# Gated cross-attention and mixture of experts: the query projection packed eight heads at a time, the second MLP layer in halves, and a new order of the side pieces

## The chip, the cores and the metric

The kernel runs on one core of one Trainium2 chip. The metric is the device time of one execution in microseconds (us), smaller is better. Each number below is from that core.

## The reference

Four batches of 512 tokens with 256 features attend to a context of 1601 rows with 192 features; 16 heads of 16 dimensions. Then a routed feed-forward layer follows. Cut to what matters:

```python
q = (layernorm(x) @ Wq + bq).reshape(B, N, 16, 16)
k = (y @ Wk + bk).reshape(B, M, 16, 16);  v = (y @ Wv + bv).reshape(B, M, 16, 16)
attn = softmax(einsum('bnhd,bmhd->bhnm', q, k) / 4)
out = einsum('bhnm,bmhd->bnhd', attn, v).reshape(B, N, 256)
x = x + tanh(g_xattn) * (relu(out @ W1 + b1) @ W2 + b2)      # W1 256x512, W2 512x256
x = x + tanh(g_ffn) * (shared expert + 2 of 8 routed experts)(layernorm(x))
```

All of it is float32.

## The kernel before

**Units and steps.** The attention works on 16 units: unit i = 4 * batch + group, where a group is four heads. A group's four heads lie on the 128 partitions in four slots of 32 partitions, 16 of them used (`HS` = 32, `HD` = 16). The keys come in 13 tiles of 128 rows (the last has 65), so there are 13 steps (i, kt) per unit, 208 steps in all, written out by hand in `step` (L622). A step holds:

- a first burst: two score matmuls of the tile after this one (`score`, L421) and two matmuls of the maxima of the unit after this one (`maximum`, L362). ScalarE takes the exponentials (`exponent`, L430), VectorE the row maxima (`reduce_max`, L373; L375 for the short last one, which falls into step kt = 10).
- the sum over values of this tile (`add_values`, L442), four heads.
- at kt = 11, where a new unit's maxima are complete, VectorE joins them (`negate`, L395), TensorE turns them (`turn_neg`, L408), and VectorE adds them to the queries (`qA_add`, L416).
- a second burst, for the other heads.
- the late work `late[s]`: side pieces that prepare the next batch or finish the last one.

The order on TensorE, ScalarE, VectorE and SyncE is the program's order (`manual_schedule`). Of PSUM's eight banks three serve the scores (`ps_sc`), three the maxima (`ps_mx`), one the sum over values, and one the side pieces (`ps_ms`, `side()`). A burst uses two of the three banks for maxima, so the second maximum of a burst needs the bank that the first reduction of the burst before it empties.

**Side pieces.** `make_q` (L289) projects the queries of one unit: the weights `wq_t` are laid out with gaps, 32 columns for a head's 16, so one unit fills 128 columns. It runs as two halves of 256 tokens, each two matmuls, and ScalarE adds the bias into `qT`. `make_k` (L306) projects keys for eight heads at once into `kd`, 16 partitions for a head, in four chunks, and `spread` (L322) brings four heads by four DMAs on SyncE's queue to their slots in one of three fixed tiles `ks`. `make_v` (L333) projects one tile of values. `normalize` (L453), `make_oT` (L475), `make_xnT` (L280) and `route` parts 0 and 1 (L518) are four transposes each; `route` part 2 is 16 small matmuls. `mlp_in` (L485) is the first layer in halves of 256 tokens, `mlp_out` (L500) the second, for 128 tokens at a time: eight matmul instructions on 256 output columns, then an addition on VectorE into `ys`. `residual` (L513) updates x and takes the statistics on VectorE. `rstd_of` (L236) starts with three small operations on VectorE and goes on on GpSimd, as `apply` (L259) does.

**The plan.** `put` (L551) assigns a piece to a step, by hand. A step that gets TensorE work is in `large`. A step with none (and not at kt = 0 or 11) has its sum over values cut into two halves (`halves`, L628), the second of them after the second burst. Last, the four warm-up pieces of values run in steps before the table, and 13 rounds of maxima of unit 0 run before the steps (L684), with the loads of `other_loads` (L197) issued in between.

After the steps the last batch is finished beside the shared expert, then the routed experts run in tiles of 128 pairs (L1040).

Of the kernel before, what the change touches and what calls it, by code (L numbers as in the profile page):

```python
# [9 lines left out]
FP = mybir.dt.float32  # L10
AF = mybir.ActivationFunctionType
# [15 lines left out]
def kernel(  # L27
# [117 lines left out]
    sp1 = xattn.enter_context(tc.tile_pool(name="sp1", bufs=1, side="right"))  # L145
    esp = xattn.enter_context(tc.tile_pool(name="esp", bufs=10, side="right"))
    wq_t = sp1.tile([P, 2, G * P], FP, name="wq_t")
    wk_t = sp1.tile([KC + 1, 2, NH * HD], FP, name="wk_t")
    wv_t = sp1.tile([KC + 1, 2, G * P], FP, name="wv_t")

# [6 lines left out]
    ctx_t = sp1.tile([KC + 1, 2, M], FP, name="ctx_t")  # L157
    nc.vector.memset(ctx_t[KC : KC + 1, 1, :], 1.0)
    ks = [sp1.tile([P, M], FP, name=f"ks_{n}") for n in range(3)]
    vs = [sp1.tile([P, NH, HS], FP, name=f"vs_{n}") for n in range(NKT + 2)]  # L160
    neg = sp1.tile([P, NTB, HPG, HS], FP, name="neg")
    for t in ks:
# [32 lines left out]
        nc.sync.dma_start(out=wv_t[:KC], in_=wv.rearrange("(c p) n -> p c n", p=KC))  # L195

    def other_loads():  # L197
        for b in range(1, B):
            load_x(b)
        for h in range(NH):  # L200
            nc.sync.dma_start(
                out=w1_t[h * HD % P : h * HD % P + HD, h * HD // P, :],
                in_=w1[h * HS : h * HS + HD, :],
            )
        nc.sync.dma_start(out=b1_t, in_=b1)
        nc.sync.dma_start(out=w2_t, in_=w2.rearrange("(c p) n -> p c n", p=P))
        nc.sync.dma_start(out=b2_t, in_=b2.partition_broadcast(P))
        nc.sync.dma_start(out=rb_t, in_=rb.partition_broadcast(P))
        nc.sync.dma_start(out=ord_t, in_=order.partition_broadcast(P))
        nc.sync.dma_start(out=wr_t, in_=wrT.rearrange("(c p) e -> p c e", p=P))  # L210
# [11 lines left out]
    mv2 = const.tile([P, NT // P, 2], FP, name="mv2")  # L222
    rstd2 = const.tile([P, NT // P], FP, name="rstd2")
    xnT, qT, qA, mxs = {}, {}, {}, {}
    kd, hid, oT, toks, ys = {}, {}, {}, {}, {}

    def side():
        return ps_ms.tile([P, S], FP, tag="ms", name="ms")
# [57 lines left out]

        return slice(0, S) if h is None else slice(h * S // 2, (h + 1) * S // 2)

    def make_q(i, h=None, ps=None):  # L289
        b, g = divmod(i, G)  # L290
        ps = side() if ps is None else ps
        n = half_of(h)
        for c in range(2):
            nc.tensor.matmul(  # L294
                ps[:, n],
                lhsT=wq_t[:, c, g * P : (g + 1) * P],
                rhs=xnT[b][:, c, n],
                start=(c == 0),
                stop=(c == 1),
            )  # L300
        if not h:
            qT[i] = sp2.tile([P, S], FP, tag="qT", name=f"qT_{i}")
            mxs[i] = sp2.tile([P, NTB, HPG, NCH], FP, tag="mxs", name=f"mxs_{i}")
        nc.scalar.activation(qT[i][:, n], ps[:, n], AF.Identity, bias=bq_t[:, g : g + 1])

    def make_k(b, h2, part, ps=None):  # L306
        if part == 0:
# [189 lines left out]
            )  # L497
        nc.scalar.activation(hid[b][:, f, n], ps[:, n], AF.Relu, bias=b1_t[:, f : f + 1])

    def mlp_out(b, t):  # L500
        ps = side()
        for f in range(NF):
            nc.tensor.matmul(  # L503
                ps[:, :H],
                lhsT=hid[b][:, f, t * P : (t + 1) * P],
                rhs=w2_t[:, f, :],
                start=(f == 0),
                stop=(f == NF - 1),
            )
        ys[b, t] = p2.tile([P, H], FP, tag="y", name=f"y_{b}_{t}")  # L510
        nc.vector.tensor_tensor(ys[b, t], ps[:, :H], b2_t, ALU.add)

    def residual(b, t):  # L513
        xt = xs[b][:, t, :]
# [34 lines left out]
    large = set()  # L549

    def put(where, i, kt, work, *args):  # L551
        if where is late and work not in (spread, load_ctx, load_expert, stats1, rstd_of, apply, residual):
            large.add(i * NKT + kt)
        where[i * NKT + kt].append(lambda: work(*args))


    for i in range(NG):
        b, g = divmod(i, G)
        nb = b + 1 if b + 1 < B else None
        if i:  # L560
            put(late, i, 1, normalize, i - 1)
        if g == 0:
            if b:
                for part, kt in enumerate((0, 2, 3, 4)):
                    put(late, i, kt, make_k, b, 1, part)
                put(late, i, 4, spread, i + 2)
                for h2 in range(2):
                    put(late, i, 5 + h2, make_oT, b - 1, h2)
            put(late, i, 7, make_q, i + 2, 0)
            put(late, i, 8, make_q, i + 2, 1)  # L570
            if b:
                for n in range(4):
                    put(late, i, 9 + n, mlp_in, b - 1, n // 2, n % 2)
            if nb:
                put(late, i, 5, load_ctx, nb)
                for t in range(NTB):
                    put(late, i, 6 + t, stats1, nb, t)
        if g == 1:
            put(late, i, 0, spread, i + 2)
            if b:  # L580
                for n, kt in enumerate((0, 2, 3, 4)):
                    put(late, i, kt, mlp_in, b - 1, 2 + n // 2, n % 2)
                for t in range(NTB):
                    put(late, i, 5 + t, mlp_out, b - 1, t)
                    put(late, i, 6 + t, residual, b - 1, t)
                put(late, i, 9, rstd_of, b - 1, mv2, rstd2, nc.gpsimd)
            put(late, i, 9, make_q, i + 2, 0)
            put(late, i, 10, make_q, i + 2, 1)
            if nb:
                put(late, i, 9, rstd_of, nb, mv1, rstd1, nc.gpsimd)  # L590
                put(late, i, 11, make_k, nb, 0, 0)
                put(late, i, 12, make_k, nb, 0, 1)
            if b:
                put(late, i, 9, apply, b - 1, mv2, rstd2, nc.gpsimd)
            if nb:
                put(late, i, 9, apply, nb, mv1, rstd1, nc.gpsimd)
                put(late, i, 8, load_expert, 0, w_sh) if b == 0 else None
        if g == 2:
            if nb:
                put(late, i, 0, make_k, nb, 0, 2)  # L600
                put(late, i, 2, make_k, nb, 0, 3)
                put(late, i, 2, spread, i + 2)
                for c in range(2):
                    put(late, i, 5 + c, make_xnT, nb, c)
                put(late, i, 8, make_q, i + 2, 0)
                put(late, i, 9, make_q, i + 2, 1)
                put(late, i, 10, make_v, nb, 0)
                put(late, i, 11, make_v, nb, 1)
                put(late, i, 12, make_q, i + 3, 0)
            if b:  # L610
                for part, kt in enumerate((3, 4, 7)):
                    put(late, i, kt, route, b - 1, part)
        if g == 3 and nb:
            put(late, i, 0, spread, i + 2)
            put(late, i, 0, make_q, i + 2, 1)
            for kt in range(2, NKT):
                put(late, i, kt, make_v, nb, kt)

    for kt in range(NKT - NCH, NKT):
        put(late, 0, kt - (NKT - NCH) - 2, make_v, 0, kt)  # L620
# [35 lines left out]
    with tc.manual_schedule(  # L656
        engines={
            mybir.EngineType.PE,
            mybir.EngineType.Activation,
            mybir.EngineType.DVE,  # L660
            mybir.EngineType.SP,
        }
    ):
        first_loads()
        for c in range(2):
            r = slice(0, KC + c)
            nc.scalar.copy(
                wk_t[r, c, :].rearrange("p (h d) -> p h d", d=HD),
                wk_slots[r, c, :].rearrange("p (h d) -> p h d", d=HS)[:, :, :HD],
            )  # L670
        for t in range(NTB):
            stats1(0, t)
        rstd_of(0, mv1, rstd1, nc.vector)
        apply(0, mv1, rstd1, nc.vector)
        for part in range(NCH):
            pool, tag = (ps_mx, "mx") if part == NCH - 1 else (ps_sc, "sc")
            make_k(0, 0, part, ps=pool.tile([P, S], FP, tag=tag, name="k0"))
        spread(0, (nc.sync, nc.scalar, nc.sync, nc.sync))
        make_k(0, 1, 0)
        for c in range(2):  # L680
            make_xnT(0, c, ps_mx.tile([P, S], FP, tag="mx", name="xnT0"))
        make_q(0, ps=ps_sc.tile([P, S], FP, tag="sc", name="q0"))
        spread(1)
        for u in range(NKT):  # L684
            banks = [(ps_mx, "mx") if j % 2 else (ps_sc, "sc") for j in range(HPG)]
            for bank in run([(maximum, reduce_max, (0, u), j, *banks[j]) for j in range(HPG)]):
                bank()
            if u == 0:
                make_q(1)
            elif u < NCH:  # L690
                make_k(0, 1, u)
            else:
                make_v(0, u - NCH)
            if u == NCH:
                spread(2)
                other_loads()
                nc.scalar.activation(tg, gt, AF.Tanh)
        for s in range(-2, LAST + 1):
            step(s)
    xattn.close()  # L700
# [515 lines left out]
```

## Time and profile before

| What | us |
|---|---|
| median of three runs | 1247.69 (1246.52 to 1248.03) |
| the profiled execution's own time | 1245.65 |
| its span, first to last instruction | 1243.9 |
| granted TensorE clock, mean | 0.999 |
| stretch of the steps | 54.2 to about 918 |
| TensorE busy in the span | 1222.9 |
| VectorE busy / ScalarE busy | 683.1 / 587.0 |

The span is 1.75 us shorter than the execution's own time, and that execution was 2.04 us faster than the median of the runs. Busy time of TensorE counts from an instruction's start to its modelled end, so matmuls that wait within a burst can still look busy; the starts of the next group tell how long a group really held the engine. In the timeline a row is: start in us, length in us, engine, line, operation, out<-in, form, count, and in brackets the idle time before it and what ended it. In the groups by line and shape a row ends with busy us, mean ns of one | idle us before.

### The profile page before, as it was taken

What the parts mean: (1) busy time and instruction counts of PE and PEld (TensorE: products, weight loads), DVE (VectorE), ACT (ScalarE), POOL (GpSimd) and SP (SyncE); (2) the same over time, 40 slices, a digit from 0 to 9 for tenths busy, and PEclk for the clock granted to TensorE, in tenths of its full rate; (3) what the DMA queues carried; (4) which work ended last, traced back from release to release, by engine and by line L of the source; (5) the groups of instructions that cost most, each with busy time, mean ns of one, the idle gap of its engine ahead of it and who ended that gap; (6) DMA issues with size and microseconds to landing.
All of it is one profiled execution on the core that took longest, in us unless ns stands there. A gap on an engine that the chain in (4) does not pass through costs nothing.

```text
span 1243.9 us, 19394 instructions
## 1 busy us (share of the span) xinstructions
PE 1222.9 (98%) x7654; PEld 544.1 (44%) x7654; DVE 683.1 (55%) x1287; ACT 587.0 (47%) x1127; POOL 129.0 (10%) x208
## 2 busy tenths in 40 slices
PE   7999999999999999999999999999999999999997
PEld 3533334333343433343434333343336656666664
DVE  5967666656666566666666665677304721121126
ACT  2265656556545555555565556545661122222220
POOL 2000110000004000000400000020000033333320
PEclk9999999999999999999999999999999999999999
DMA  5312000002000100120010001000047011111106
GB/s 125 103 41 65 1 15 15 1 1 54 14 2 4 29 14 1 27 41 1 1 31 15 1 1 17 11 1 18 1 152 271 1 35 39 46 46 40 44 23 207
DMA packets 30752, 48.29 MB, mean 39 GB/s; under 512 B 5247, under 2 KB 21505, under 8 KB 30662
## 3 DMA queue, kind: packets, MB, share of 16 engines
q1 hardware_dynamic: 26628, 38.14, 11.7%
q0 software_dynamic: 3504, 8.40, 2.1%
q8 instruction: 62, 1.02, 0.3%
q10 hardware_dynamic: 530, 0.50, 0.1%
q14 instruction: 28, 0.23, 0.1%
HBM read 32.86 MB, written 8.78 MB: 33 GB/s over the span
## 4 chain that ended last, share of the span: by engine, by line
PE 94%; DVE 2%; issue 1%; DMA 1%; ACT 0%; POOL 0%; SPq 0%; POOLq 0%; DVEq 0%; ACTq 0%
PE sc L421 32%; PE av L442 17%; PE gp L998 5%; PE up L998 5%; PE y_ps L1016 5%; PE mx L362 4%; PE ms L339 4%; PE ms L313 3%; PE ms L491 3%; PE ms L294 3%; PE ms L503 2%; PE up L721 1%; PE gp L721 1%; PE th L1009 1%; PE op L744 1%
## 5 line engine op out<-in xcount | busy, mean ns | idle before, releaser
L373 DVE TENSOR_REDUCE mxs<-mx 128x1 f32<-128x512 f32 x744 | 479.8, 685 | 251.1 <-PE mx L362 247.3
L430 ACT ACTIVATE es<-sc 128x512 f32<-128x512 f32 x804 | 437.7, 594 | 340.9 <-PE mx L362 291.3
L362 PE MATMUL mx<-ks,qT 32*128 32x512 f32 (+1 forms) x1984 | 480.6, 549 | 0.0
L421 PE MATMUL sc<-qA,ks 32*128 32x512 f32 x1608 | 467.6, 637 | 0.8 <-DVE qA L416 0.8
L421 PEld LDWEIGHTS sc<-qA,ks 32*128 32x128 f32 x1608 | 131.2, 179 | 221.8 <-issue 165.3
L442 PE MATMUL av<-es,vs 128*32 128x512 f32 (+2 forms) x1864 | 227.8, 559 | 0.1
L362 PEld LDWEIGHTS mx<-ks,qT 32*128 32x128 f32 x1984 | 164.7, 183 | 4.0 <-issue 1.9
L442 PEld LDWEIGHTS av<-es,vs 128*32 128x32 f32 (+1 forms) x1864 | 37.1, 108 | 166.2 <-issue 161.2
L1052 DVE TENSOR_TENSOR hid<-sg,up 128x512 f32<-128x512 f32 x35 | 24.1, 688 | 124.2 <-PE up L998 124.2
L244 POOL TENSOR_SCALAR var<-var 128x4 f32<-128x4 f32 x6 | 1.4, 238 | 782.8 <-DVE first L241 782.8
L1050 ACT ACTIVATE sg<-gp 128x512 f32<-128x512 f32 x35 | 20.9, 598 | 103.8 <-PE gp L998 103.8
L998 PE MATMUL gp<-w_all,xT 128*128 x140 | 66.0, 594 | 0.9 <-ACT xT L994 0.9
L1016 PE MATMUL y_ps<-w_all,hT 128*128 x280 | 66.2, 379 | 0.0
L998 PE MATMUL up<-w_all,xT 128*128 x140 | 65.9, 593 | 0.0
L339 PE MATMUL ms<-wv_t,ctx_t 96*128 96x256 f32 (+1 forms) x208 | 58.7, 404 | 0.1
L1016 PEld LDWEIGHTS y_ps<-w_all,hT 128*128 128x128 f32 x280 | 50.6, 190 | 5.9 <-issue 0.5
L339 PEld LDWEIGHTS ms<-wv_t,ctx_t 96*128 96x128 f32 (+1 forms) x208 | 34.5, 185 | 37.9 <-issue 27.3
L1025 POOL DMA_INDIRECT rows_y<-y,dest x35 | 35.6, 1017 | 131.0 <-DVE y L1024 131.0
L313 PE MATMUL ms<-ctx_t,wk_t 96*128 96x401 f32 (+3 forms) x112 | 45.1, 524 | 0.0
L978 POOL DMA_INDIRECT xg<-rows_x,token x38 | 39.2, 1031 | 48.1 <-DVE token L962 36.7
L737 ACT ACTIVATE sg<-gp 128x512 f32<-128x512 f32 x16 | 9.6, 597 | 62.7 <-PE gp L721 52.5
L375 DVE TENSOR_REDUCE mxs<-mx 128x4 f32<-128x260 f32 x62 | 23.8, 424 | 26.4 <-PE sc L421 22.6
(165 smaller groups left out, 943.9 us busy)
## 6 DMA issues: line engine op xcount, KB each, us to landing
ks<-kd SPq DMA_DIRECT2D x63, 100.1 KB, 3.2
w_all<-in_wgT SPq DMA_DIRECT2D x8, 512.0 KB, 11.1
w_all<-in_wuT SPq DMA_DIRECT2D x8, 512.0 KB, 10.0
w_all<-in_wdT SPq DMA_DIRECT2D x8, 512.0 KB, 11.2
w_all<-rows_y SPq DMA_DIRECT2D x8, 512.0 KB, 8.4
ctx_t<-in_ctxT SPq DMA_DIRECT2D x3, 1200.8 KB, 8.1
xb<-in_x SPq DMA_DIRECT2D x4, 512.0 KB, 6.2
rows_x<-xn SPq DMA_DIRECT2D x4, 512.0 KB, 3.4
```

Source lines behind the costliest of these rows:

```text
L294: nc.tensor.matmul(ps[:, n], lhsT=wq_t[:, c, g * P : (g + 1) * P], rhs=xnT[b][:, c, n], start=(c == 0), stop=(c == 1),)
L313: nc.tensor.matmul(ps[:, :n], lhsT=wk_t[r, c, h2 * P : (h2 + 1) * P], rhs=ctx_t[r, c, o : o + n], start=(c == 0), stop=(c == 1),)
L339: nc.tensor.matmul(ps[:n, : NH * HD], lhsT=ctx_t[r, c, o : o + n], rhs=heads[r, c, :, :HD], start=(c == 0), stop=(c == 1),)
L362: nc.tensor.matmul(ps[:, n * REST : (n + 1) * REST] if last else ps, lhsT=qT[i][slot_of(j), qb * P : (qb + 1) * P], rhs=ks[i % 3][slot_of( ...
L373: nc.vector.tensor_reduce(mxs[i][:, qb, j, c : c + 1], ps, AX.X, ALU.max)
L421: nc.tensor.matmul(ps[:n, :], lhsT=ks[i % 3][r, o : o + n], rhs=qA[i][r, :], start=True, stop=True)
L430: nc.scalar.activation(es[(i * NKT + kt) % 2, j][:n], ps[:n], AF.Exp, scale=SCALE)
L442: nc.tensor.matmul(av[i][j * HS : (j + 1) * HS, cols], lhsT=v_of(b, kt)[:n, g * HPG + j, :], rhs=es[(i * NKT + kt) % 2, j][:n, cols], star ...
L491: nc.tensor.matmul(ps[:, n], lhsT=w1_t[:, c, f * P : (f + 1) * P], rhs=oT[b][:, c, n], start=(c == 0), stop=(c == 1),)
L978: nc.gpsimd.indirect_dma_start(out=xg[i % 4], out_offset=None, in_=rows_x, in_offset=bass.IndirectOffsetOnAxis(ap=token[:, i : i + 1], axi ...
L998: nc.tensor.matmul(ps, lhsT=xT[i][:, c, :], rhs=w_flat[:, bass.ds(owners[i] + (off + c) * I, I)], start=(c == 0), stop=(c == 1),)
L1016: nc.tensor.matmul(ps, lhsT=hT2[i][:, f, :], rhs=w_flat[:, bass.ds(owners[i] + 4 * I + f * H, H)], start=(f == 0), stop=(f == NI - 1),)
```

## The change

The weights of the queries are also kept without gaps: `wq_d`, 256 columns for 16 heads, is made from `wq_t` by two ScalarE copies in the warm-up, and `bq_d`, its bias, is loaded by two more DMAs. Units 0 and 1 are still projected from `wq_t` (`first_q`). All others go through `make_q(b, h2, h)`, which projects eight heads at once into `qd`, and `spread_q`, which sends four heads by four DMAs on SyncE's queue to their slots in one of two fixed tiles `qs`. The gaps in `qs` keep the zeros that `first_q` wrote. `mlp_out` runs in two halves of 128 output columns where the plan calls it (the last batch, after the steps, keeps it whole). The plan of side pieces of a batch is written anew.

```diff
-    def make_q(i, h=None, ps=None):
-        b, g = divmod(i, G)
...
+    def make_q(b, h2, h):
+
+        ps = side()
         n = half_of(h)
         for c in range(2):
             nc.tensor.matmul(
                 ps[:, n],
-                lhsT=wq_t[:, c, g * P : (g + 1) * P],
+                lhsT=wq_d[:, c, h2 * P : (h2 + 1) * P],
                 rhs=xnT[b][:, c, n],
...
+    def spread_q(i):
+        b, g = divmod(i, G)
+        home_of(i)
+        for j in range(HPG):
+            r = (g % 2 * HPG + j) * HD
+            nc.sync.dma_start(
+                out=qT[i][j * HS : j * HS + HD, :], in_=qd[b, g // 2][r : r + HD, :]
+            )
...
-    def mlp_out(b, t):
+    def mlp_out(b, t, h=None):
         ps = side()
+        n = slice(0, H) if h is None else slice(h * H // 2, (h + 1) * H // 2)
         for f in range(NF):
             nc.tensor.matmul(
-                ps[:, :H],
+                ps[:, n],
                 lhsT=hid[b][:, f, t * P : (t + 1) * P],
-                rhs=w2_t[:, f, :],
+                rhs=w2_t[:, f, n],
...
-        nc.vector.tensor_tensor(ys[b, t], ps[:, :H], b2_t, ALU.add)
+        if not h:
+            ys[b, t] = p2.tile([P, H], FP, tag="y", name=f"y_{b}_{t}")
+        nc.vector.tensor_tensor(ys[b, t][:, n], ps[:, n], b2_t[:, n], ALU.add)
...
+    for b in range(B):
+        i = b * G
         nb = b + 1 if b + 1 < B else None
+        mlp = [(mlp_in, b - 1, n // 2, n % 2) for n in range(2 * NF)]
+        outs = [(mlp_out, b - 1, n // 2, n % 2) for n in range(2 * NTB)]
...
+        put_all(i, (7, 8), [(make_q, b, 1, h) for h in range(2)])
+        put(late, i, 8, spread_q, i + 2)
+        put(late, i + 1, 0, spread, i + 3)
+        put(late, i + 1, 2, spread_q, i + 3)
+        if b and nb:
+            put_all(i, (9, 10, 11, 12), mlp[:4])
+            put_all(i + 1, (0, 2, 3, 4), mlp[4:])
+            at = [(i + 1, 5 + n) for n in range(2 * NTB)]
+        elif b:
+            put_all(i, (9, 10, 12), mlp[:3])
+            put_all(i + 1, (0, 2, 3, 4, 5), mlp[3:])
+            at = [(i + 1, kt) for kt in (6, 7, 8, 9, 10, 12)] + [(i + 2, 0), (i + 2, 2)]
+        if b:
+            for n, (k, kt) in enumerate(at):
+                put(late, k, kt, *outs[n])
+                if n % 2:
+                    put(late, *divmod(k * NKT + kt + 1, NKT), residual, b - 1, n // 2)
+            k, kt = divmod(k * NKT + kt + 1, NKT)
+            put(late, k, kt, rstd_of, b - 1, mv2, rstd2, nc.gpsimd)
+            put(late, k, kt, apply, b - 1, mv2, rstd2, nc.gpsimd)
+            put_all(i + 2, (9, 10, 12) if nb else (8, 9, 10), [(route, b - 1, n) for n in range(3)])
...
+            put(late, i + 1, 3, rstd_of, nb, mv1, rstd1, nc.gpsimd)
+            put(late, i + 1, 3, apply, nb, mv1, rstd1, nc.gpsimd)
...
+            put_all(i + 2, (0, 2, 3, 4), [(make_k, nb, 0, part) for part in range(NCH)])
+            put(late, i + 2, 4, spread, i + 4)
+            put_all(i + 2, (5, 6), [(make_xnT, nb, c) for c in range(2)])
+            put_all(i + 2, (7, 8), [(make_q, nb, 0, h) for h in range(2)])
+            put(late, i + 2, 8, spread_q, i + 4)
+            put(late, i + 3, 0, spread, i + 5)
+            put(late, i + 3, 2, spread_q, i + 5)
...
+                for c in range(2):
+                    nc.scalar.copy(
+                        wq_d[:, c, :].rearrange("p (h d) -> p h d", d=HD),
+                        wq_t[:, c, :].rearrange("p (h d) -> p h d", d=HS)[:, :, :HD],
+                    )
```

Values keep their 13 pieces a batch: in batches 1 and 2 the first one moves from (i + 2, 10) to (i + 2, 11) and the second from there to (i + 3, 0); in batch 0 they fill (i + 2, 9), (i + 2, 10) and all of unit i + 3 but steps 1 and 11.

## The prediction

> **What bounds the kernel.** I read the page's busy table first, then the chain that ended last, then the groups by line and shape, then the timeline of TensorE in steps of each kind.
>
> ```profile
> PE 1222.9 (98%) x7654; PEld 544.1 (44%) x7654; DVE 683.1 (55%) x1287; ACT 587.0 (47%) x1127; POOL 129.0 (10%) x208
> ...
> PE 94%; DVE 2%; issue 1%; DMA 1%; ACT 0%; POOL 0%; SPq 0%; POOLq 0%; DVEq 0%; ACTq 0%
> ```
>
> TensorE (PE) is busy 98% and holds 94% of the chain: time goes where its instructions go, unless a wait hides inside a burst. So I price whole steps, by starts in its timeline. One step of unit 5 (rows of L362 left out):
>
> ```profile
> 354.46 0.69 PE L421 MATMUL sc<-qA,ks 32*128 32x512 f32 x1
> ...
> 355.53 1.06 PE L442 MATMUL av<-es,vs 128*32 128x512 f32 x8
> 356.52 0.69 PE L421 MATMUL sc<-qA,ks 32*128 32x512 f32 x1
> ...
> 357.60 1.99 PE L503 MATMUL ms<-w_t,hid 128*128 128x256 f32 x8
> 359.52 0.69 PE L421 MATMUL sc<-qA,ks 32*128 32x512 f32 x1
> ```
>
> A burst takes 1.07 us (354.46 to 355.53), the sum over values 1.00, the second burst 1.07, the piece of the second layer 1.92. The fixed part is 3.14; what the late slot costs comes on top. By the same reading: a query, value or first-layer piece costs 1.06 (L294: 372.78 to 373.84), keys 1.55, router logits 1.88, four transposes 0.59 plus a stall of 0.27 in the next burst. An empty slot, whose sum over values is halved, makes a step of 3.57 (127.35 to 130.92), so it costs 0.43, all stall.
>
> The stalls have one mechanism. Reductions start 1.20 after their burst (366.65 to 367.85). The next burst's second maximum needs the bank of the first of them, which is free after 0.69 more and some 0.08. Bursts are 2.07 apart with 1.00 between them, so VectorE may be 0.1 late for nothing; each further us is a us of TensorE. The profile shows the price where VectorE (DVE) gets late work ahead of its reductions:
>
> ```profile
> 374.12 0.48 DVE L515 SCALAR_TENSOR_TENSOR xb<-y,tg,xb 128x256 f32<-128x256 f32 x1
> 374.63 0.43 DVE L216 BATCH_NORM_STATS2 st<-xb 128x6 f32<-128x256 f32 x1
> ...
> 376.23 0.17 DVE L242 TENSOR_SCALAR first<-first 128x4 int32<-128x4 int32 x1
> ...
> 376.31 0.76 DVE L375 TENSOR_REDUCE mxs<-mx 128x4 f32<-128x260 f32 x2
> ```
>
> After a residual and two `rstd_of`, reductions due at 373.84 + 1.20 = 375.04 start at 376.31, and the next burst takes 1.91 instead of 1.06. The rule gives 1.27 + 1.20 + 0.42 (these are short) + 0.08 - 2.07 = 0.90 for the measured 0.85; at (13, 10), 0.82 late, 0.45 for 0.40.
>
> **The query pieces.** Counting the plans: 28 pieces become 14, of the same form (128 by 128 weights, 256 columns), so 1.06 each stays. Fourteen go: 14.8 us of TensorE.
>
> **The second layer in halves.** Twelve pieces of 1.92 become 24, each eight instructions of 128 columns. This form is not in the trace.
>
> ```profile
> L294 PE MATMUL ms<-xnT,wq_t 128*128 128x256 f32 x112 | 31.7, 405 | 0.0
> L503 PE MATMUL ms<-w_t,hid 128*128 128x256 f32 x128 | 31.5, 389 | 0.0
> ...
> L531 PE MATMUL ms<-wr_t,x2T 128*128 128x8 f32 x64 | 7.7, 256 | 0.0
> ```
>
> Four instructions take 1.06, eight 1.92: 0.215 each and 0.20 fixed. The router's sixteen move 8 columns only and take 1.88, (1.88 - 0.20) / 16 = 0.105 each: that is the loading of 128 weight columns. Moving 128 columns is half of 0.215, 0.107. If the load runs beside the move, a half costs 0.20 + 8 x 0.11 = 1.08; if not, 0.20 + 8 x 0.212 = 1.90; below 0.20 + 8 x 0.105 = 1.04 it cannot go, since the loads themselves remain. I take 1.08: at 256 columns the load is wholly hidden, and the transposes, 128 weight columns against 128 moved, take (0.59 - 0.20) / 4 = 0.10 each. So 24 x 1.08 - 12 x 1.92 = 2.9 us are added.
>
> The Trainium skill (TensorE: Matmul & The Clock Gate, "Back-to-back issue gap") speaks against this: in a stream of load and matmul pairs the spacing is set by both, about 81 ns at 128 columns where the move alone has 56. No row here has that form in float32; the 25 ns more, carried over to each instruction, are an estimate of 4.8 us less gain.
>
> **The slots.** Pieces fall by 14 and rise by 12, so the row is two shorter, and an empty slot pays only where a stall doesn't take its place. At kt = 11 it hardly pays: unit 0 has it empty, and the burst at 107.75 takes 1.95 instead of 1.07, since scores wait for `qA_add`. The new plan leaves kt = 11 empty in units 0 to 3, 12 and 13 (before: 0 and 13). Summing steps by these rows, before against after, with 1.08 for a half:
>
> - batch 0, (1, 9) to (3, 12): 76.3 against 75.1, saves 1.2. Two query pieces and more go, but three emptied turning steps give most back.
> - batch 1, (5, 5) to (7, 0): four query pieces go (4.24), eight halves for four wholes add 0.96, and the stall of 0.85 goes. Saves 4.1; batch 2 alike, 4.2 (its stall is 0.92).
> - batch 3, (12, 11) to (14, 11): 96.4 against 94.0, saves 2.4.
>
> Together 11.9.
>
> **What is late next.** Whole pieces gave VectorE 1.92 to do a residual (0.48, 0.43, 0.18) and an addition of 0.41; halves give 1.08. In the row of 367.85 reductions, residual and addition end 2.66 after the first reduction starts; with half an addition (0.27) that is about 2.5, so 3.70 after the burst began. The next reductions are due at 1.07 + 1.08 + 1.20 = 3.35: 0.35 late, a stall of 0.25. This holds after (5, 7), (5, 11), (6, 0) and their likes in batch 2, and (13, 8) and (14, 0): eight times, 2.0. After (5, 9) and (13, 10), beside the short reductions, it is nothing. At (14, 3), a residual and an `rstd_of` in an empty step: VectorE is done at 2.49 + 1.07 + 0.60 = 4.2 where 3.0 is due: 1.15. Costs: 3.15. `rstd_of` alone, at (1, 3) and (5, 3), ends at 3.1, 0.1 late at most: nothing.
>
> **What costs nothing.** The 56 DMAs of `spread_q`: their issue takes SyncE 0.54 each and landing 3.3 by the rows of `spread`, which moves three times as much. The last issue starts 1.9 after ScalarE's bias (0.6 after the matmuls), lands 3.3 later: 5.8, and the first user, (i, 11), comes two steps later, 8.4 (7.0 in unit 0). Cover left: 1.2 at the least. Behind them on SyncE wait `spread` of the next unit and the router's store, neither due before a unit has passed. The order frees the tiles in time: `qs[i % 2]` was last read at (i - 1, 11). The two bias loads go ahead of loads needed at 85 us and later, issued by 51. The two ScalarE copies (0.41 each, from L667's) lie in the warm-up, where a round is four reductions of VectorE, 2.6, and ScalarE has one copy of 0.37. Without that cover they would cost 0.8. Everything after 918 is unchanged.
>
> **The sum.** 11.9 - 3.15 = 8.8. The profiled execution, 1245.65, becomes 1236.9; the median stands 2.04 above it, so 1238.9. A measurement of this kernel tells about 0.2% (2.5 us) from no change.
>
> **The rivals.**
>
> - *Weight loads not hidden at 128 columns*: each half 1.90, 24 x 0.82 = 19.7 more, 1258.6: slower. It decides from 1.08 + 8.8 / 24 = 1.45 a half, 156 ns an instruction. For it: load and move are then equally long, with no slack. Against: the transposes' 0.10. Chance 0.08. *In part*: a quarter of each load's 0.105 shows, 24 x 8 x 0.026 = 5.0 less gain, 1243.9; chance 0.10. (The skill's page above would land beside this one.)
> - *VectorE becomes the bound in the second layer's steps*: each of the twelve residuals costs what the worst row showed, 0.85, and (14, 3) 1.15 on top of eleven: 11 x 0.85 + 1.15 = 10.5, leaving 1.4: 1246.3, no change. For it: reductions, residual and half an addition fill 3.9 of 4.2 in such a step. Against: the next step has no residual, and the lateness by the row is 0.35, not 1.3. Chance 0.10.
> - *The spread is late*: four transfers one after another, 0.6 + 4 x 3.3 = 13.8, are 5.4 late at seven places: 38 us, 1277. Against: `spread`'s four land within 2 us of each other. Chance 0.03.
> - *More*: the stalls of 3.15 are absorbed: 1235.7. Chance 0.07.
>
> The forecast itself, 1236 to 1242, has 0.62. Range: 1233 to 1248, with the two slow cases outside (0.11). Faster: 0.62 + 0.10 + 0.07 = 0.79; same 0.10; slower 0.11.
>
> **What would show it.** The second layer's group with 192 instructions of 128 columns, and 1.08 from a half's start to the next burst; bursts of 1.3 after the eight residuals named, and one of over 2 after (14, 3); queries at 56 instructions of 256 columns; no wait of TensorE on a DMA into `qs`. Halves over 1.45, or bursts of 1.9 after each residual, would make it wrong.

## The result, and the profile after

| What | before | after |
|---|---|---|
| median of six runs each on one chip, us | 1247.53 (1246.14 to 1248.03) | 1236.38 (1235.44 to 1239.71) |
| ratio | | 0.992, 95% interval 0.9908 to 0.9931 |
| the profiled execution's own time | 1245.65 | 1239.71 |
| its span | 1243.9 | 1237.9 |
| granted TensorE clock, mean | 0.999 | 0.995 |

Faster, by 11.2 in the medians where 8.8 was forecast; 1236.38 lies 2.5 below the forecast of 1238.9 and in its range.

In some executions TensorE's clock falls to half for some 3.4 us, which costs some 1.6 each time (last section), and the profile of after has two such falls; so whatever is finer than some 3 us is compared below by summing the steps of the traces, from the first step's start to the last one's end, less what falls took from them.

The busy table and the chain that ended last, of after:

```profile
PE 1216.8 (98%) x7686; PEld 542.6 (44%) x7686; DVE 682.9 (55%) x1299; ACT 581.3 (47%) x1115; POOL 129.6 (10%) x208
...
DVE 1%; DMA 0%; PE 0%; issue 0%
```

TensorE's busy time fell by 6.1, and the span by 6.0: it is the bound as before. The chain no longer shows it, because the walk back from the last instruction ends early at a transfer (`w_all<-rows_y`); a chain whose shares add up to 1% says nothing of the rest. TensorE's instructions rose by 32: 56 of queries gone, 96 of the second layer turned into 192, and 8 gone because one step fewer has its sum over values halved. The groups by line and shape:

```profile
L540 PE MATMUL ms<-w_t,hid 128*128 128x128 f32 x192 | 27.8, 288 | 0.0
...
L320 PE MATMUL ms<-xnT,wq_d 128*128 128x256 f32 x56 | 15.8, 405 | 0.0
```

The queries' 112 instructions are 56, of the same 405 ns each. The sum of the second layer's records, 27.8, is not what it holds of the engine: records of a pipelined engine overlap. For that the starts are read. Two halves in unit 5, rows of other lines left out:

```profile
358.74 1.16 PE L540 MATMUL ms<-w_t,hid 128*128 128x128 f32 x8
359.83 0.69 PE L457 MATMUL sc<-qA,ks 32*128 32x512 f32 x1
...
362.97 1.16 PE L540 MATMUL ms<-w_t,hid 128*128 128x128 f32 x8
364.06 0.69 PE L457 MATMUL sc<-qA,ks 32*128 32x512 f32 x1
```

A half holds TensorE from 358.74 to 359.83: 1.09, and so do all 24.

Summed by stretches, in us, with the clock fall in the steps of after (1.58, at 666.4) taken out:

| stretch | before | after | saved | forecast, with its stalls |
|---|---|---|---|---|
| (1, 9) to (3, 12) | 126.95 | 125.90 | 1.05 | 1.2 |
| units 4 to 7 | 227.51 | 223.68 | 3.83 | 3.35 |
| units 8 to 11 | 227.58 | 223.68 | 3.90 | 3.45 |
| (12, 0) to (14, 11) | 160.44 | 158.98 | 1.46 | 0.75 |
| all steps | 865.33 | 855.09 | 10.24 | 8.75 |

The other stretches are equal to 0.01. Of the two spans, 6.0 apart, the steps account for 10.24 less the 1.58 of the fall, and the time after them for 0.3; the first step began 3.03 later in after (57.20 for 54.17). That is no cost of the change: the kernel with the packed queries alone, which has the same two copies and loads ahead of the steps, began at 54.14. In the 13 profiles of all kernels here the steps start at 54.1 to 57.6. The first matmul on a loaded tile starts at 7.6 to 8.4. From there to the first step five profiles take 46.1 to 46.7; the six in which the clock falls once at 24 to 25 us take 48.9 to 49.1; and two, whose clock rises to full only at 13.5 and 17.3 us where those five have 11.9 to 13.3, take 47.6 and 49.0. Kernels with the same warm-up as after stand in each of these groups, so the late start is not the kernel's.

**The stalls.** VectorE after (5, 7), which has a residual behind a half:

```profile
363.10 1.29 DVE L409 TENSOR_REDUCE mxs<-mx 128x1 f32<-128x512 f32 x2 [0.78 <-PE mx L398]
364.31 0.48 DVE L553 SCALAR_TENSOR_TENSOR xb<-y,tg,xb 128x256 f32<-128x256 f32 x1
...
365.38 0.26 DVE L549 TENSOR_TENSOR y<-ms,b_t 128x128 f32<-128x128 f32 x1
365.55 1.28 DVE L409 TENSOR_REDUCE mxs<-mx 128x1 f32<-128x512 f32 x2
```

From the first reduction to the end of residual and addition pass 2.45, so the next reductions start at 365.55; the burst began at 364.06, so they were due at 365.26. They are 0.29 late, and the second burst of the step takes 1.22 instead of 1.07: a stall of 0.15. At (14, 3), where the empty step has a residual and an `rstd_of`, VectorE first and then TensorE:

```profile
849.60 1.29 DVE L409 TENSOR_REDUCE mxs<-mx 128x1 f32<-128x512 f32 x2 [0.35 <-PE mx L398]
850.80 0.48 DVE L553 SCALAR_TENSOR_TENSOR xb<-y,tg,xb 128x256 f32<-128x256 f32 x1
...
852.47 0.17 DVE L250 TENSOR_SCALAR first<-first 128x4 int32<-128x4 int32 x1
852.55 1.28 DVE L409 TENSOR_REDUCE mxs<-mx 128x1 f32<-128x512 f32 x2
```

```profile
851.97 0.69 PE L457 MATMUL sc<-qA,ks 32*128 32x512 f32 x1
...
854.34 0.64 PE L478 MATMUL av<-es,vs 128*32 128x256 f32 x8
```

The reductions were due at 850.33 + 1.20 = 851.53 and start at 852.55. The burst that waits for their bank, from 851.97, holds TensorE for 2.37; in the empty steps without such work it is 1.36. So 1.02 is lost here.

### The profile page after: what moved, and what is told of

The parts are those of the page before. It is cut to its first block, busy times and chain, and to the rows that moved or that the text cites. A ratio compares the mean times of both kernels' runs of the same rounds, so it can differ in the third digit from the quotient of the medians.

```text
span 1237.9 us, 19528 instructions
## 1 busy us (share of the span) xinstructions
PE 1216.8 (98%) x7686; PEld 542.6 (44%) x7686; DVE 682.9 (55%) x1299; ACT 581.3 (47%) x1115; POOL 129.6 (10%) x208
## 5 line engine op out<-in xcount | busy, mean ns | idle before, releaser
L398 PE MATMUL mx<-ks,qs 32*128 32x512 f32 (+1 forms) x1984 | 483.9, 550 | 0.0
L478 PE MATMUL av<-es,vs 128*32 128x512 f32 (+3 forms) x1856 | 228.1, 562 | 0.2
L398 PEld LDWEIGHTS mx<-ks,qs 32*128 32x128 f32 x1984 | 165.3, 184 | 3.0 <-issue 1.4
```

Source lines behind the costliest of these rows:

```text
L398: nc.tensor.matmul(ps[:, n * REST : (n + 1) * REST] if last else ps, lhsT=qT[i][slot_of(j), qb * P : (qb + 1) * P], rhs=ks[i % 3][slot_of( ...
L478: nc.tensor.matmul(av[i][j * HS : (j + 1) * HS, cols], lhsT=v_of(b, kt)[:n, g * HPG + j, :], rhs=es[(i * NKT + kt) % 2, j][:n, cols], star ...
```

## The experiments

The theory: TensorE's time is the sum of its steps, so the gain is the sum of what the three edits take from the steps (fewer query pieces, shorter pieces behind residuals, the slots), less the stalls where VectorE is late; the spread is free because it has two steps of room. Rivals were tied to each run. Eleven runs were made: nine new kernels, the kernel after once more, and the last new one once more. Step sums are set against 865.33 of before and 855.09 of after.

### The packed queries alone

`e1_q_alone`: `make_q` and `spread_q` of after with the plan of before, the second layer whole; what before did with the freed slots is left out, and the router's logits and the queries change places in two steps. In short:

```diff
-            put(late, i, 7, make_q, i + 2, 0)
-            put(late, i, 8, make_q, i + 2, 1)
+            put(late, i, 7, make_q, b, 1, 0)
+            put(late, i, 8, make_q, b, 1, 1)
+            put(late, i, 8, spread_q, i + 2)
...
-            put(late, i, 9, make_q, i + 2, 0)
-            put(late, i, 10, make_q, i + 2, 1)
...
+            put(late, i, 2, spread_q, i + 2)
```

> The packed queries and their spread alone, in the plan of before (the second layer whole, query pieces taken out of its row, router logits and queries swapped in two steps). Theory of the forecast, slots priced by rows: fourteen query pieces leave mostly empty slots, which give 0.63 each at a halved step, 0.2 at kt = 0 and nothing where VectorE is late; sum 5.8 us under the kernel before. Rival (TensorE work counts in full): 14 x 1.06 = 14.8 us under it. Rival (the plan and the halves made the gain): within 1 us of before.

Measured: 1241.95 median (ratio 0.9961, 0.9948 to 0.9973); steps 859.40, 5.93 less than before. So packing gives somewhat over half of the gain, far less than 14 x 1.06 = 14.8, since an emptied slot pays only 0.63 (4.20 to 3.57), and less where work on VectorE falls into it. The place is (5, 9), empty here, with a residual and two `rstd_of`:

```profile
371.72 0.48 DVE L553 SCALAR_TENSOR_TENSOR xb<-y,tg,xb 128x256 f32<-128x256 f32 x1
...
373.83 0.17 DVE L250 TENSOR_SCALAR first<-first 128x4 int32<-128x4 int32 x1
373.90 0.76 DVE L411 TENSOR_REDUCE mxs<-mx 128x4 f32<-128x260 f32 x2
```

Between two pairs of reductions VectorE does 2.2 of other work, and the second burst of (5, 10) takes 2.54; in after it takes 1.06, in before 1.91.

### The second layer whole, in the new order

`e2_whole`: a whole piece where the first half was, nothing where the second was.

```diff
-                put(late, k, kt, *outs[n])
-                if n % 2:
+                if n % 2 == 0:
+                    put(late, k, kt, mlp_out, b - 1, n // 2)
+                else:
```

> The changed kernel with the second layer whole again, each at the slot of its first half, the slot of the second half left empty. Theory: a whole piece and an empty slot cost 5.06 + 3.57 = 8.63 where two halves cost 8.46, twelve times 0.17 = 2.0, less the stalls after residuals of 0.7: about 1.2 us over the changed kernel. Rival (halving is what makes the gain): 5 us or more over it.

Measured: 1240.23 (0.9954, 0.9938 to 0.9971); steps 857.03, so the halves are worth 1.94 where 1.2 was expected. The rows alone give 12 x (1.92 + 0.43 - 2 x 1.09) = 2.0, and the stalls after halves (0.7 in all, see below) do go; but an empty step ahead of a burst costs something too: the first bursts of (6, 0) and (10, 0) take 1.21 and 1.22 for 1.07, and (13, 12) and (14, 0) together 0.15 more than the rows say. So the stalls come back elsewhere, in the main. It is far under the rival's 5: halves are no cure of a large stall, they fill twelve slots that otherwise stand empty at 0.43 each.

### Two halves in one slot

`e6_two_in_one`: as the last, but the whole piece runs as two runs of eight instructions of 128 columns, in one step.

```diff
-                    put(late, k, kt, mlp_out, b - 1, n // 2)
+                    put(late, k, kt, mlp_out, b - 1, n // 2, 2)
```

> The kernel e2_whole with each second-layer piece computed as two runs of 128 columns one after the other in one slot (16 instructions, one addition after them). Theory (a piece costs 0.20 fixed and an instruction of 128 columns 0.111): 0.20 + 16 x 0.111 = 1.98 a piece against 1.92 whole, 0.7 us over e2_whole in the stretch of the steps. Rival (narrow instructions carry the cost that the halves show, 1.09 each): 2.18 a piece, 3.1 us over it.

Measured: 1240.69 (one run); each of the twelve pieces holds TensorE for 1.98, against 1.92 whole. With two halves at 1.09 it would be 2.18. So the cost is 0.20 once and 16 x 0.111: the fixed part is paid once for a piece, however many runs of eight it has, and each instruction of 128 columns takes 0.111. This is the reading that the price of 1.08 was built on.

### One start of the reciprocal root for two

`e3_rstd_joined`: for batches 1 and 2, the `rstd_of` of the next batch's normalisation is put back beside that of the last one's residual, in one step.

> The changed kernel with the first norm of the next batch (rstd_of, apply) put back to the step of the second norm of the last one, as before, in batches 1 and 2. Theory (each us that VectorE is late beyond 0.1 is a us of TensorE): three small operations, 0.6, more ahead of the reductions after (6, 0) and (10, 0): second bursts of (6, 1) and (10, 1) go from 1.26 to 1.86, 1.2 us in all. Rival (the keys' piece of 1.55 hides it): no change.

Measured: 1239.03 (0.9929, 0.9912 to 0.9946); steps 857.48, less a fall of 1.59 is 855.89: 0.80 more than after, where 1.2 was expected. The cost sits where it was looked for: the second burst of (6, 1) takes 1.70 for 1.26, while (6, 2) gives back 0.08. The new plan's parting of the two is worth 0.8.

### The queries later, with no room for the spread

`e5_queries_late`: in batches 1 to 3 the queries of heads 8 to 15 change places with first-layer pieces, so that `spread_q` starts at (i, 10), one step before its first user.

```diff
-        put_all(i, (7, 8), [(make_q, b, 1, h) for h in range(2)])
-        put(late, i, 8, spread_q, i + 2)
+        put_all(i, (9, 10) if b else (7, 8), [(make_q, b, 1, h) for h in range(2)])
+        put(late, i, 10 if b else 8, spread_q, i + 2)
```

> The changed kernel with the two pieces of packed queries of units 4, 8 and 12 moved from (i, 7) and (i, 8) to (i, 9) and (i, 10), two first-layer pieces taking their places, so that no step lies between the bias and the first use at (i, 11). Theory (the spread costs nothing because two steps cover it): in the changed kernel the last of the four transfers lands 4.4 us after the query matmuls end, and the third 3.7; the first burst of (i, 11) grows from 1.07 by about 4 at each of three places, 12 us in all, more if the clock falls in the gap. Rival (the transfers are never on the path): no change.

Measured: 1257.28 (one run); steps 876.36, 21.3 more than after. At (4, 11), all engines, and below it the wait of TensorE:

```profile
318.25 1.13 PE L320 MATMUL ms<-xnT,wq_d 128*128 128x256 f32 x4
...
319.31 1.07 PE L457 MATMUL sc<-qA,ks 32*65 32x512 f32 x2
319.42 0.47 ACT L329 ACTIVATE qd<-ms,bq_d 128x256 f32<-128x256 f32 x1
319.92 2.41 SPq L338 DMA_DIRECT2D qs<-qd  x4
...
323.14 0.66 PE L398 MATMUL mx<-ks,qs 32*128 32x512 f32 x1 [2.76 <-issue]
```

```profile
PE mx L398 <- DMA qs<-qd: 2.8, 1, 2.8
```

The maxima of the next unit read `qs` and wait until its transfers have landed. (In the view of waits, only one of the three stops is put down to the transfer; two stand as "issue", 5.5 together. TensorE's first row after the stop tells more than the label.) A transfer lands 1.95 after its issue, so the last of four, issued at 321.74, is there at 323.69: 4.4 after the matmuls ended at 319.31. Three such stops add 7.6, 6.0 and 7.7. The clock is at half after each of them, for 6.8, 3.4 and 6.8; half of that time, 8.5, is an estimate of what the clock takes, and it leaves 12.7 for the stops themselves. So the spread is no longer free as soon as its room is gone: the rival that it is never on the path falls.

### Filled turning steps and a split residual

`e4_fill_split`: the steps at kt = 11 that the new plan leaves empty in batches 0 and 3 get a piece, and the statistics of a residual move one step behind it, the `rstd_of` one more.

```diff
-            put_all(i, (9, 10, 12), mlp[:3])
+            put_all(i, (9, 10, 11), mlp[:3])
...
-            k, kt = divmod(k * NKT + kt + 1, NKT)
+                    put(late, *divmod(k * NKT + kt + 2, NKT), stats2, b - 1, n // 2)
+            k, kt = divmod(k * NKT + kt + 3, NKT)
```

> The changed kernel with the turning steps kt = 11 of units 2, 3, 12 and 13 filled from kt = 12 (or 10), which is left empty in their place, and with the statistics of a residual one step after it and rstd_of one step later still. Theory: a filled turning step saves the 0.94 that the next burst waits and costs 1.19, the emptied one saves 0.6 to 1.5: 0.3 to 0.5 each, 1.6 together; the split takes the stalls after residuals, 0.7, and 1.0 at (14, 3): 3.2 us under the changed kernel. Rival (turning and the piece share one bank, so filling gives nothing): 1.7 under it.

Measured: 1237.76 (0.9928, 0.9915 to 0.9941); steps 854.45, less a fall of 1.60 is 852.85: 2.24 less than after, between theory and rival. All stalls after halves are gone and the burst of 2.38 at (14, 4) is 1.36. Two things fell short. At (6, 2) and (10, 2) the statistics now meet a normalisation, 5.24 for 4.76, which takes back all that the split gains in batches 1 and 2. And the four turning steps give 0.39 once and 0.25 three times, 1.1 together where 1.6 was reckoned: (12, 11) and (12, 12) take 3.62 and 5.12 when the first is empty, 4.78 and 3.57 when it is filled, but the first burst after the emptied step, at (3, 0), (4, 0), (13, 0) and (14, 0), takes 1.21 to 1.22 and not 1.07.

### Each of the two alone

`e10_fill_alone` and `e11_split_alone` have one edit each of the last kernel.

> Only the emptied turning steps are filled again, in batches 0 and 3; the residual stays in one piece. From the steps of the two kernels that had both edits: refilling (2, 11) saves 0.38, (3, 11) 0.24, (12, 11) and (13, 11) 0.25 each, so the steps are 1.1 shorter than those of the changed kernel without its clock fall (855.1): 854.0. As to the end of the kernel: theory A (the scatter of the last experts' rows lands 1.9 later because of something in the plan, the later statistics) has it land 2.4 after its start here and the tail 324.1 long; theory B (it varies from run to run) allows 326.0 here too; theory C (it comes with the filled steps) demands 326.0 here.

> Only the residual is split, with its statistics one step later and the reciprocal root one more; the turning steps stay empty. The stalls of 0.15, 0.11 and 0.19 after halves go in batches 1 and 2, (6, 2) and (10, 2) lose 0.48 each where statistics meet a normalisation, and the burst of 2.38 at (14, 4) goes (1.0): the steps are about 1.1 shorter than 855.1, 854.0. Theory A has the tail at 326.0 here, with the last scatter landing 4.3 after its start; theory B allows either; theory C has 324.1.

Measured: 1236.90 and 1241.09 (one run each). Steps: filling alone 854.56, 0.53 less than after instead of 1.1; splitting alone 857.44, less two falls of some 1.6 each, 854.2, 0.8 less. Together they gave 2.24, some 0.9 more than the sum. The reason is in two places. Filling alone makes (13, 12) an empty step that has a residual, and the second burst of (14, 0) takes 1.70; with the residual split it takes 1.07. Splitting alone lets the statistics meet a normalisation at (14, 2), whose second burst takes 1.35; with the second layer moved by the filling it takes 1.07. As to the end of the kernel, theory A falls: with the split alone the tail is 324.3, with the fill alone 326.2.

### All of it

`e8_best`: the last two edits, the statistics kept off the normalisation's step, the last pieces of the second layer of batch 2 one step earlier, and the router's logits of batch 2 in two halves. `e9_after_again` is the kernel after, unchanged, on the same chip.

```diff
+    def after_of(k, kt):
+        k, kt = divmod(k * NKT + kt + 1, NKT)
+        return k, kt + (kt == 1)
...
+                put_all(i + 2, (7, 8), [(route, b - 1, n) for n in range(2)])
+                put_all(i + 2, (9, 10), [(route, b - 1, 2, h) for h in range(2)])
```

> e4_fill_split with the statistics after the last residual moved past the step of normalize, the second layer of batch 2 one step earlier, and its router logits in two halves of eight instructions. Theory: 0.28 twice, and 0.5 in batch 3 (an empty slot less, an extra fixed 0.20): 1.0 us under e4_fill_split in the stretch of the steps, 3.3 under the changed kernel; and the clock keeps full speed after (14, 10), where e3_rstd_joined and e4_fill_split lost 1.6 each, because no 1.9 us of eight-column matmuls stands before the gap of the turning. Rival (the falls of the clock don't depend on the logits): it falls there again.

> The changed kernel unaltered, on the same chip as e8_best, as its measure: 9.8 to 10.5 us under the kernel before where neither run shows a fall of the clock.

Measured: 1236.72 (1236.48 to 1237.95; 0.9917, 0.9903 to 0.993) and 1237.11 (1235.68 to 1239.12; 0.9914, 0.9899 to 0.9929). The steps are 851.83, 3.26 less than after's as reckoned, but the time is not. In its profile 1.9 come back at the end of the kernel, where VectorE waits for the routed rows:

```profile
DVE xb L1178 <- DMA w_all<-rows_y: 1.9, 2, 1.1
```

The last scatter of rows started 296.0 after the steps' end, as in after, but landed 4.3 later instead of 2.4. The same kernel was run once more:

> The kernel with filled turning steps, split residual, its statistics kept off the normalisation's step, and the router's logits of the last batch in two halves, once more. The steps measured 851.8, 3.3 below the changed kernel's without its clock fall. If the 1.9 at the end is this kernel's own (theories A and C), the tail is 326.0 again and the gain that can be had over the changed kernel is 1.4; if it varies from run to run (theory B), a tail of 324.1 can come, and runs at a clock of 0.998 or more should reach 1232 to 1233 (1235.6 less 3.3).

Measured: 1236.71 (1234.87 to 1237.62; 0.9917, 0.9903 to 0.993). The tail is 324.1 here, and the scatter took 2.5: theories A and C fall, the end varies from run to run of one kernel. The steps are 855.02 with two falls of the clock of 3.2 together, so 851.8 again. The 1232 to 1233 that theory B gave for a clock of 0.998 or more was not to be seen: no run had such a clock, the fastest, 1234.87, had 0.997. The version that is 3.3 shorter in its steps beats the kernel before, but is not told apart from the kernel after by its times: what the falls, the warm-up and the last scatter add varies by as much.

## Why the prediction was right

- *Fourteen query pieces less, 1.06 each*: right; 56 instructions, same 405 ns.
- *A half costs 1.08*: 1.09, all 24. The rival of loads that are not hidden (1.90) and the one in part are refuted. An instruction of 128 columns takes (1.09 - 0.20) / 8 = 0.111, of which 0.107 is the move by half of 256 columns; a quarter of each load shown would have been 0.133. The Trainium skill's page (TensorE: Matmul & The Clock Gate, "Back-to-back issue gap") has 81 ns for 56 at 128 columns, 25 more. Here the excess over the move is 4 ns, so that surplus is not found in this float32 form.
- *The slots save 11.9*: 10.24 measured plus the stalls of 1.7 (below) make 11.9. The division by edits, which the prediction did not give: queries alone 5.9, taken from before; halves 1.9, taken from after; what is left, 2.4, goes to the new order, which was not run by itself.
- *VectorE is late eight times for 0.25, 2.0 in all*: the term that was mis-sized. The places are right, all eight, the sizes not: the bursts take 1.18 to 1.26 where 1.3 was said. Measured are 0.15, 0.11 and 0.19 in batches 1 and 2 each, 0.14 twice in batch 3, and 0.19 and 0.14 of that are given back at once, because the next step's burst, which waits for a normalisation (1.34), starts later anyway and needs 1.15 and 1.20. Net 0.15 + 0.11 twice and 0.14: 0.7 instead of 2.0. The chain of residual and addition took 2.45, not 2.5, and some 0.14 of lateness is free, not 0.1. With a term this close to its threshold, 0.1 us less of lateness is nearly half of the cost.
- *1.15 at (14, 3)*: 1.02.
- *The spread costs nothing, with 1.2 of cover at the least*: right, with more cover: issue 0.58 each, landing 1.95 and not 3.3. At (8, 8) the matmuls end at 536.91, the last transfer lands at 541.28, and the first user starts at 545.29: 4.0 left (in unit 0, where the steps between are shorter, 2.6). No wait of TensorE on `qs<-qd` is in the trace of after; with the room taken away there is one.
- *Copies and bias loads free*: the two copies take 0.70 together in the warm-up, and kernels with them begin their steps as early as before, 54.1.
- *The sum*: 8.8 forecast, 10.24 by the steps; the 1.5 between is the stalls. The medians differ by 11.15, but runs at a granted clock of 0.999 by 9.8 (before 1245.6, median of 16; after 1235.8, of 4). So what the medians show beyond that goes with how many runs of each kernel had a lower clock; that it is nothing else is not shown, since only the profiled runs tell when the clock fell. The forecast of the median took over 2.04 between the profiled execution and the median of before; after's profiled execution lies 3.33 above its median, so this step was no property of the kernel, and that the median came within 2.5 is in part luck.

## What to carry to other kernels

On an engine that is never idle, price a removed piece by the step that it leaves, not by its own length: here 14.8 of matmuls removed gave 5.9, since the emptied slot fills with waits for the other engines. Splitting a piece pays where pieces are fewer than slots and the split costs less than an empty slot: here 2 x 1.09 - 1.92 = 0.26 against 0.43. And don't put a residual into an empty step. A transfer that replaces work on the full engine is free as long as its whole way (issue, landing) fits ahead of its first reader; here it needed 4.4 and had 8.4 (7.0 in unit 0), and with its reader right behind the matmuls it cost 4.2 a time, and the clock besides.

## What the runs showed of the hardware

**The clock falls although the profile shows TensorE busy throughout, and only at certain phases.** Two windows of after on either side of 666.38:

```profile
core 0: us, PE busy (x) PEld busy (x) DVE busy (x) ACT busy (x) POOL busy (x), PEclk, DMA share, GB/s
...
662.97:666.36 3.39, 3.39 (x31) 1.99 (x24) 2.96 (x5) 1.91 (x4) 0.00 (x0) 1.00 0.36 62
666.39:669.77 3.38, 3.38 (x19) 0.99 (x18) 1.12 (x3) 0.97 (x2) 0.00 (x0) 0.50 0.05 10
```

Both are full by busy time. The first one holds most of the router's sixteen matmuls on 8 columns (1.88 at full clock, from 664.69); the second ran at half clock, and (10, 12) and (11, 0) together lost 1.58. All falls lie on one grid within an execution: those of after at 24.668 and 666.374 are 641.706 apart, 188.0 times 3.4133. The Trainium skill (TensorE: Matmul & The Clock Gate, "What's actually happening") has a free-running window of 4096 cycles at 1.2 GHz, 3413 ns; grid and length agree. Its idle windows don't describe the fall in the middle, which had none; the falls of the kernel with late queries, after stops of 4.5 with 1.74 of work, are of its kind.

In the 13 profiles there are 37 router pieces in the steps. Nine began 0.94 to 1.75 after a grid point, and eight of these were followed by a fall at the next one; the ninth, at 1.59 in (6, 9) of the kernel with the packed queries alone, was not. Of the 28 others none was. That is a relation, not a proof: that the 8 columns are what the clock's monitor counts as little work was not tried by itself. If it holds, a piece of many small matmuls costs 1.88 and, by its phase, in about a quarter of the cases another 1.6; the four half pieces of 0.99 had no fall behind them, though one of them began at 1.58.

**A scatter of the same rows landed after 2.4 or 4.3.** It was 4.3 in the three profiles in which it began at 1204.6 to 1204.8, and 2.4 to 2.5 in the other ten, in which it began at 1206.6 or later. In all of them it began 295.9 to 296.1 after the end of the steps. Why stays open; it decided 1.9 us of the end.
